# LoRA masks by four products of 32 rows with a constant, in a four-layer transformer kernel

## The chip, the cores and the metric

The kernel runs on one core of a Trainium2 chip. The metric is the device time of one execution in microseconds (us), the median over runs. The engines are called as in the profile: PE (TensorE, matrix products), PEld (its weight loads), DVE (VectorE), ACT (ScalarE), POOL (GpSimd) and SP (SyncE, which issues the DMAs).

## The reference

The reference is four layers; each adds a gated attention-like part and a gated feed-forward part to `x` of 32 x 64 tokens by 256 features (2048 tokens). What matters here is the feed-forward part of the first layer, a gated network with routed LoRA experts (8 experts, the best 2 for each token, rank 16):

```python
gate_base, up_base = xf @ Wg.T, xf @ Wu.T            # 256 -> 704
base_out = jax.nn.silu(gate_base) * up_base @ Wd.T
probs = jax.nn.softmax(xf @ Wr.T, axis=-1)           # 8 experts
topw, topi = jax.lax.top_k(probs, 2)
expert_w = jnp.sum(jax.nn.one_hot(topi, 8) * topw[..., None], axis=1)
for e in range(8):                                   # a scan
    g_lora = xf @ Ag[e].T @ Bg[e].T * 2.0            # rank 16
    u_lora = xf @ Au[e].T @ Bu[e].T * 2.0
    h = jax.nn.silu(gate_base + g_lora) * (up_base + u_lora)
    acc += (h @ Ad[e].T @ Bd[e].T * 2.0) * expert_w[:, e, None]
x = x + jnp.tanh(g_ffn[0]) * (base_out + acc)
```

The kernel computes only the two chosen experts of each token: all 8 x 16 = 128 inner rows of `Ag` and `Au` are computed in one product, and a mask over these 128 rows keeps the rows of the first or of the second expert. A second pair of masks carries the weights for the way out.

## The kernel before

All activations `x` stay on the core as 16 tiles of 128 tokens. The layers are eight blocks: `block0` (a recurrence, by scans on DVE), `block1` (the routed network above), `block2` (a convolution), `block3` (a ternary network), `blocks45` and `block6`, `block7`. Blocks 0 and 1 run together: they work on chunks of two, two, four, four and four tiles (`CHUNKS`), and `program` draws pieces of block 0 between the steps of block 1. Up to the end of block 3 the order of the instructions is set by a planner that works from estimated costs, with the order in the program as priority and the free buffers as a limit; from `blocks45` on PE, DVE, ACT and POOL keep the order in which the program is written.

In block 1 a generator `head` prepares a chunk: layer norm, transposes to `xf` (features on partitions, tokens along the row), and `route`, which gives `sel`. `sel` has tokens on partitions and, for each tile, 4 x 8 values: for every expert whether it is the first (`s` = 0) or the second choice, and the two weights. `head` then builds `mt`, four masks of 128 rows by n x 128 tokens, where a row belongs to expert row // 16. Here POOL copies the 32 values of a tile 16 times each to 512 (`ex`, line 411), PE turns them in four transposes (line 415) into a PSUM tile `pm`, and ACT copies it to `mt` (line 416). `ex` has one buffer; `pm` comes from the pool `c.aux` with tag "a", which has two buffers and is used by the other transposes of blocks 0 and 1 as well. Then the products `pz` (line 423, tag "a" too) give the inner rows of gate and up, and DVE multiplies them with the masks to `z` (line 426). The head of the next chunk is stepped by `ahead` in the last eight steps of a chunk; the head of the first chunk is done at once.

The chunk itself: `gated` takes `pg` and `pu` (line 462 for the base, 465 for the LoRA part of each choice) through silu on ACT (468) and a product on DVE (469); then `pa` (509, 524), `po` (515, 532) and `finish` (537, 542), which adds to `x`. The masks come in again in line 527.

Other lines the prediction names: block 0's `bv` (278), scans (282, 287) and `y` (294) with reciprocals (299), its transposes (181); the load of `con`, a table of constants (1792), and of block 1's weights `l0f` (1763, 1764); `_norm` (167) writes `xn`, also in `blocks45`, where `xn` of tile 0 comes from one pool and those of the other tiles from another. In block 6, lines 1559 and 1569 are products of 32-row strips.

Of the kernel before, what the change touches and what calls it, by code (L numbers as in the profile page):

```python
# [17 lines left out]
F32 = mybir.dt.float32  # L18
# [8 lines left out]
P = 128  # L27
# [20 lines left out]
def _offsets(sizes):  # L48
    out, at = {}, 0
    for name, n in sizes:  # L50
        out[name] = (at, at + n)
        at += n
    return out, at
# [11 lines left out]
L2X, L2X_N = _offsets([("wq", 512), ("wo", 512), ("wk", 512), ("wv", 512), ("mask", NT * S), ("bk", 2), ("bq", 2)])  # L65
ROWS, ROWS_N = _offsets([("bv", D), ("bo", D), ("gb", HID), ("vb", HID), ("ob", D)])
CON, CON_N = _offsets(
    [("cos", 256), ("sin", 256), ("had", P), ("pairs", P), ("half", 2), ("tri", 64), ("odd", 2)]
)
L3X, L3X_N = _offsets([("wq", 256), ("wk", 256), ("wv", 128), ("wo", 128), ("bias", 4), ("bo", 1), ("bv", 1)])  # L70

# [1 line left out]
def _v(t, off, name):  # L73
    a, b = off[name]
    return t[:, a:b]
# [52 lines left out]
def _stats(c, pool, i0=0, n=NT, bufs=1, here=False):  # L128

    mv = pool.tile([P, max(n, 4), 2], F32, tag="ln_mv", name="ln_mv", bufs=bufs)[:, :n]  # L130
    for j in range(n):
        _mean(c, pool, mv[:, j, :], i0 + j, here)
    return mv, _inverse(c, pool, mv, "ln", bufs), i0
# [29 lines left out]
def _norm(c, pool, ln, i, bufs=4):  # L163
    mv, rs, i0 = ln
    j = i - i0
    xn = pool.tile([P, D], F32, tag="xn", name="xn", bufs=bufs)
    c.nc.vector.tensor_scalar(xn, c.x[:, i, :], mv[:, j, 0:1], rs[:, j : j + 1], ALU.subtract, ALU.mult)  # L167
    return xn
# [7 lines left out]
def _turned(c, xns, ps, tag):  # L176
    out = []
    for hf in range(2):
        pt = ps.tile([P, 512], F32, tag=tag, name="pt")
        for q in range(len(xns)):  # L180
            c.nc.tensor.transpose(pt[:, q * P : (q + 1) * P], xns[q][:, hf * P : (hf + 1) * P], c.ident)
        out.append(pt)
    return out
# [148 lines left out]
def block1(c):  # L332
# [5 lines left out]
    nc = c.nc  # L338
# [6 lines left out]
    au = _v(w, L0F, "au").rearrange("p (k e) -> p k e", k=2)  # L345
    ad = _v(w, L0F, "ad").rearrange("p (f e) -> p f e", e=P)
    wr = _v(w, L0F, "wr").rearrange("p (k e) -> p k e", k=2)
    bg, bu, bd = _v(w, L0F, "bg"), _v(w, L0F, "bu"), _v(w, L0F, "bd")
    E = 8
    with ExitStack() as es:  # L350
        sm = es.enter_context(c.tc.tile_pool(name="sm1", bufs=1))
        ps = es.enter_context(c.tc.tile_pool(name="ps1", bufs=6, space=PSUM))
        ph = c.aux
        hp = es.enter_context(c.tc.tile_pool(name="hp1", bufs=1))
        tp = es.enter_context(c.tc.tile_pool(name="tp1", bufs=2))
# [37 lines left out]
        def head(i0, n):  # L393

            ln = _stats(c, sm, i0, n, bufs=2)
            yield
            xns = [_norm(c, sm, ln, i0 + q) for q in range(n)]
            yield
            N = n * P
            xf = tp.tile([P, 2, 512], F32, tag="xf", name="xf")  # L400
            pts = _turned(c, xns, ph, "a")
            nc.scalar.copy(xf[:, 0, :N], pts[0][:, :N])
            nc.scalar.copy(xf[:, 1, :N], pts[1][:, :N])
            yield
            sel = route(xf, n)
            yield
            mt = hp.tile([P, 4, 512], F32, tag="mt", name="mt", bufs=2)
            for q in range(n):
                ex = tp.tile([P, 4 * E, 16], F32, tag="ex", name="ex", bufs=1)
                src = sel[:, q, :, :].rearrange("p a e -> p (a e)")  # L410
                nc.gpsimd.tensor_copy(ex, src.unsqueeze(2).to_broadcast([P, 4 * E, 16]))
                exf = ex.rearrange("p a r -> p (a r)")
                pm = ph.tile([P, 4, P], F32, tag="a", name="pm")
                for a in range(4):
                    nc.tensor.transpose(pm[:, a, :], exf[:, a * P : (a + 1) * P], c.ident)
                nc.scalar.copy(mt[:, :, q * P : (q + 1) * P], pm)
                if q % 2:
                    yield
            z = {}
            for m, wt in (("g", ag), ("u", au)):  # L420
                pz = ph.tile([P, 512], F32, tag="a", name="pz")
                for k in range(2):
                    nc.tensor.matmul(pz[:, :N], wt[:, k, :], xf[:, k, :N], start=k == 0, stop=k == 1)
                for s in range(2):
                    z[m, s] = hp.tile([P, 512], F32, tag=f"z{m}{s}", name=f"z{m}{s}", bufs=2)
                    nc.vector.scalar_tensor_tensor(z[m, s][:, :N], pz[:, :N], 2.0, mt[:, s, :N], ALU.mult, ALU.mult)
                z[m, 2] = hp.tile([P, 512], F32, tag=f"z{m}2", name=f"z{m}2", bufs=2)
                nc.gpsimd.tensor_tensor(z[m, 2][:, :N], z[m, 0][:, :N], z[m, 1][:, :N], ALU.add)
            ready.append((xf, mt, z))
            yield  # L430
# [3 lines left out]
        for _ in head(*CHUNKS[0]):  # L434
            pass
        for t, (i0, n) in enumerate(CHUNKS):
            N = n * P
            xf, mt, z = ready.pop(0)
            nxt = head(*CHUNKS[t + 1]) if t + 1 < len(CHUNKS) else None
            step = 0  # L440

# [71 lines left out]
            for q in range(n):  # L513
                for f in range(NF):
                    ins = nc.tensor.matmul(  # L515
                        pos[q % 2][:, q // 2], h[2][:, f, q * P : (q + 1) * P], wd[:, f, :],
                        start=f == 0 and q < 2, stop=False, skip_group_check=True,
# [3 lines left out]
                if q == 1:  # L521
                    for s in range(2):
                        rows = slice(s * S, (s + 1) * S)
# [6 lines left out]
            for q in range(n):  # L530
                rows, tc = slice(q % 2 * S, (q % 2 + 1) * S), slice(q * P, (q + 1) * P)
# [403 lines left out]
def blocks45(c, kw):  # L935
# [6 lines left out]
    nc = c.nc  # L942
# [4 lines left out]
    half = _v(c.con, CON, "half")  # L947
    pairs = _v(c.con, CON, "pairs")
# [13 lines left out]
    with ExitStack() as es:  # L962
        es4 = es.enter_context(ExitStack())
        sm4 = es4.enter_context(c.tc.tile_pool(name="sm4", bufs=1, side="right"))
        t4 = es4.enter_context(c.tc.tile_pool(name="te4", bufs=1, side="right"))
# [9 lines left out]
        lns, more = [_stats(c, sm4, 0, 4, bufs=2)], []  # L975
# [58 lines left out]
        @op  # L1034
        def xn(a):
            a.x = c.x[:, a.i, :]
            a.xn = _norm(c, t4, lns[a.i // 4], a.i, bufs=2)

        @op
        def gbo(a):  # L1040
# [377 lines left out]
        t4 = es4.enter_context(c.tc.tile_pool(name="tp4", bufs=2, side="right"))  # L1418
# [317 lines left out]
def program(tc, a, out):  # L1736
    nc = tc.nc
    with ExitStack() as es:
# [45 lines left out]


        first, second = block0(c), block1(c)
        next(first)
        early, conv_w = ExitStack(), ExitStack()
# [105 lines left out]
def _constants():  # L1894

    con = np.zeros((P, CON_N), np.float32)
    inv = (np.float32(1.0) / np.float32(10000.0) ** (np.arange(0, 8, 2, dtype=np.float32) / np.float32(8))).astype(np.float32)
    f = (np.arange(D, dtype=np.float32)[:, None] * inv[None, :]).astype(np.float64)
    a = CON["cos"][0]
    b = CON["sin"][0]  # L1900
    o = CON["odd"][0]
    for j in range(4):
        for h in range(2):
            rows = slice(32 * j + 8 * h, 32 * j + 8 * (h + 1))
            con[rows, a : a + D] = np.cos(f[:, np.arange(8) % 4]).T
            con[rows, b : b + D] = np.sin(f[:, np.arange(8) % 4]).T * np.repeat([-1.0, 1.0], 4)[:, None]
            con[32 * j + 16 + h, a : a + D] = 1.0
            con[rows, o + h] = 1.0
            con[32 * j + 16 + h, o + h] = 1.0
    had = np.ones((1, 1), np.float32)  # L1910
    while had.shape[0] < P:
        had = np.block([[had, had], [had, -had]])
    con[:, slice(*CON["had"])] = had
    p = np.arange(P)
    con[:, slice(*CON["pairs"])] = p[:, None] // 64 == p[None, :] // 64
    con[:, slice(*CON["half"])] = p[:, None] % 32 // 16 == np.arange(2)[None, :]
    e = np.arange(8)
    con[:, slice(*CON["tri"])] = (e[None, :] < e[:, None]).reshape(1, 64)
    return con

# [20 lines left out]
def _layout(i):  # L1941
# [37 lines left out]
    out["wu"] = np.concatenate([i["L0_xattn_w"].reshape(2, P).T, i["L0_xattn_u"].reshape(2, P).T], axis=1)  # L1979
    out["l3f"] = np.concatenate([_chunks(i["L3_ffn_W1"].T), _chunks(i["L3_ffn_W3"].T), _chunks(i["L3_ffn_W2"].T)], axis=1)  # L1980
    out["con"] = _constants()
    return {n: np.ascontiguousarray(v) for n, v in out.items()}

# [13 lines left out]
```

## Time and profile before

| | |
|---|---|
| median of 3 runs | 1341.95 us (1341.44 to 1345.03) |
| the profiled execution | 1339.78 us, of which the span of the instructions is 1337.9 us |
| granted TensorE clock, mean | 0.973 |
| `ex` copies, POOL, line 411 | 16, 804 ns mean (602 to 1423 ns) |
| mask transposes, PE, line 415 | 64, 273 ns median from start to end, pipelined |
| `mt` copies, ACT, line 416 | 16, 586 ns median |
| last products of block 1 (line 537) | start at 360.61 us |

Times in the profile are microseconds from the start of the span. A line of a timeline has the start, the length, the engine, the source line, the operation, what it writes and reads with shapes, how many, and in square brackets the engine's idle time before it and who ended it. Matmuls overlap in the array, so the time that PE gives to one is seen from start to start, not from its length. An f32 product is two instructions; a transpose is one.

### The profile page before, as it was taken

To read this page: it belongs to the slowest core of one execution; us is meant where nothing else is said; L and a number is where in the kernel's file an instruction comes from. 1 tells how busy PE (TensorE), PEld (TensorE's weight loads), DVE (VectorE), ACT (ScalarE), POOL (GpSimd) and SP (SyncE) were. 2 spreads that over 40 slices of the span, in tenths; PEclk is the share of its full clock that TensorE was granted. 3 is DMA by queue.
4 is the path that set the end of the run, shared out by engine and by line. 5 is a ranking of instruction groups with operands and counts; after the bars stand their busy time and mean duration, and the time that the engine had idled before them with its cause. 6 is when DMAs were issued, how large, how long until landed. Compare 5 with 4: busy or idle time off the path is not lost.

```text
span 1337.9 us, 21457 instructions
## 1 busy us (share of the span) xinstructions
PE 1193.0 (89%) x8342; PEld 722.0 (54%) x8342; DVE 906.7 (68%) x2175; ACT 618.6 (46%) x1046; POOL 460.3 (34%) x505
## 2 busy tenths in 40 slices
PE   0789899899999999987878976799999999999999
PEld 0667345354533367765656653455555555555665
DVE  6588777645349897558999996587787887532111
ACT  2563634322131154657989981455555555511110
POOL 3332606210113233325777775233234335000000
PEclk9899999999999998989999996899999999999999
DMA  6000000100142120000000010110000000000000
GB/s 216 20 1 16 1 0 1 63 1 1 46 175 95 49 87 1 1 1 1 2 2 2 1 65 1 37 59 1 2 1 1 2 1 1 1 8 9 16 16 16
DMA packets 10294, 34.14 MB, mean 26 GB/s; under 512 B 1360, under 2 KB 5968, under 8 KB 8528
## 3 DMA queue, kind: packets, MB, share of 16 engines
q1 hardware_dynamic: 10192, 32.76, 6.9%
q8 instruction: 66, 1.08, 0.3%
q14 instruction: 36, 0.29, 0.1%
HBM read 30.66 MB, written 2.10 MB: 24 GB/s over the span
## 4 chain that ended last, share of the span: by engine, by line
PE 58%; DVE 27%; POOL 5%; ACT 4%; issue 4%; DMA 2%; SPq 0%; DVEq 0%; POOLq 0%; ACTq 0%
PE pw L1559 6%; PE po L1582 5%; PE pp L1569 4%; PE po L1731 4%; PE pu L1721 4%; PE pg L1721 4%; PE pc L610 3%; PE pu L462 2%; PE pg L462 2%; PE pu L465 2%; PE pa L509 2%; DVE xn L167 2%; PE po L515 2%; PE pg L465 2%; PE pp L1502 1%
## 5 line engine op out<-in xcount | busy, mean ns | idle before, releaser
L1575 DVE TENSOR_REDUCE mx<-pp 128x4 f32<-128x1024 f32 x128 | 155.9, 1218 | 40.7 <-PE pp L1569 40.3
L1561 ACT ACTIVATE e<-pw 128x1024 f32<-128x1024 f32 x128 | 130.9, 1024 | 111.1 <-PE pw L1559 67.0
L1559 PE MATMUL pw<-qs,kb 32*128 32x256 f32 x1024 | 144.5, 402 | 7.5 <-DVE qs L1546 4.4
L1569 PE MATMUL pp<-kb,q 32*128 32x512 f32 x512 | 147.3, 658 | 4.3 <-POOL q L1530 4.0
L1559 PEld LDWEIGHTS pw<-qs,kb 32*128 32x128 f32 x1024 | 87.2, 185 | 51.9 <-issue 29.2
L468 ACT ACTIVATE sg<-pg 128x512 f32<-128x512 f32 (+1 forms) x75 | 37.8, 512 | 116.6 <-PE pg L462 51.1
L610 PE MATMUL pc<-xw,wb 64*64 64x512 f32 x768 | 90.3, 601 | 0.2 <-DVE x L542 0.2
L1724 DVE TENSOR_TENSOR h<-pu,sg 128x512 f32<-128x512 f32 x32 | 22.1, 692 | 80.8 <-PE pu L1721 80.8
L1723 ACT ACTIVATE sg<-pg 128x512 f32<-128x512 f32 x32 | 19.1, 597 | 122.8 <-PE pg L1721 122.7
L469 DVE TENSOR_TENSOR h<-pu,sg 128x512 f32<-128x512 f32 (+1 forms) x75 | 42.5, 573 | 48.1 <-PE pu L462 29.4
L1524 POOL TENSOR_TENSOR k<-t,t 128x512 f32<-128x512 f32 x16 | 20.3, 1267 | 147.9 <-DVE t L1509 147.9
L1582 PE MATMUL po<-e,va 128*32 128x256 f32 x1024 | 69.2, 388 | 1.8 <-ACT e L1561 1.8
L764 POOL TENSOR_TENSOR acc<-acc,sq 128x512 f32<-128x512 f32 x28 | 38.3, 1369 | 68.6 <-ACT sq L763 67.3
L1721 PE MATMUL pg<-xf,wa 128*128 128x512 f32 x128 | 60.3, 592 | 0.0
L1721 PE MATMUL pu<-xf,wa 128*128 128x512 f32 x128 | 60.3, 592 | 0.0
L610 PEld LDWEIGHTS pc<-xw,wb 64*64 64x64 f32 x768 | 30.1, 133 | 53.4 <-issue 52.6
L1731 PE MATMUL po<-hb,h 128*128 128x256 f32 x256 | 55.9, 379 | 0.0
L1731 PEld LDWEIGHTS po<-hb,h 128*128 128x128 f32 x256 | 48.6, 190 | 8.3 <-issue 1.9
L110 DVE BATCH_NORM_STATS2 ln_st<-x 128x6 f32<-128x256 f32 x112 | 44.4, 409 | 10.9 <-POOL x L1611 7.2
L1582 PEld LDWEIGHTS po<-e,va 128*32 128x32 f32 x1024 | 26.9, 110 | 44.0 <-issue 17.4
L1509 DVE SCALAR_TENSOR_TENSOR t<-pp,wb,con 128x512 f32<-128x512 f32 x64 | 45.0, 744 | 8.3 <-PE pp L1502 8.3
L1527 POOL TENSOR_SCALAR kb<-k,con 128x512 f32<-128x512 f32 x32 | 49.7, 1564 | 1.6
(342 smaller groups left out, 2947.0 us busy)
## 6 DMA issues: line engine op xcount, KB each, us to landing
w<-in_l2f SPq DMA_DIRECT2D x12, 512.0 KB, 3.9
wa<-in_l0f SPq DMA_DIRECT2D x2, 1828.0 KB, 12.7
wa<-in_l1f SPq DMA_DIRECT2D x2, 1536.0 KB, 9.3
wa<-in_l3f SPq DMA_DIRECT2D x2, 1536.0 KB, 8.0
wb<-in_conv SPq DMA_DIRECT2D x1, 2048.0 KB, 7.5
ctx<-in_ctxT SPq DMA_DIRECT2D x2, 1024.0 KB, 6.0
ctx<-in_ctxN SPq DMA_DIRECT2D x2, 1024.0 KB, 5.9
out<-x SPq DMA_DIRECT2D x16, 128.0 KB, 1.7
```

Of the source, the lines that this page charges most:

```text
L462: nc.tensor.matmul(p, wt[:, k, fc], xf[:, k, :N], start=k == 0, stop=False, skip_group_check=True)
L465: nc.tensor.matmul(p, wt[:, fc], z[m, s][:, :N], start=False, stop=s == 1, skip_group_check=True)
L610: nc.tensor.matmul(pcs[h][to], w[rows, k, m, h, :], xw[rows, k, h, :, Z - m : Z - m + 32], start=m == 0, stop=m == Z)
L1509: nc.vector.scalar_tensor_tensor(t[r], pp[:, :, r, :], bias[:, n, r : r + 1], f, ALU.add, ALU.mult)
L1527: nc.gpsimd.tensor_scalar(kb[:, :, h, :], k, odd[:, h : h + 1], None, ALU.mult)
L1559: nc.tensor.matmul(pw[:, jj, k, :], w.k[rows, h, k * P : (k + 1) * P], w.qs[rows, :], start=True, stop=True)
L1561: nc.scalar.activation(e, pw, AF.Exp, scale=scale)
L1569: nc.tensor.matmul(pp[:, jj], p.q[rows, t * P : (t + 1) * P], p.k[rows], start=True, stop=True)
L1575: nc.vector.tensor_reduce(p.mx[:, t, i0 : i0 + 2, 16:18], pp, AX.X, ALU.max, negate=True)
L1582: nc.tensor.matmul(po[strip(j), :], a.v[:, k, 2 * j + h, :], a.e[h, j][:, k, :], start=k == 0, stop=k == 1)
L1721: nc.tensor.matmul(p, wt[:, k, fc], xf[:, k, :], start=k == 0, stop=k == 1)
L1731: nc.tensor.matmul(po, h[:, f, q * P : (q + 1) * P], c.w2h[:, f, :], start=f == 0, stop=f == NH - 1)
```

## The change

The 32 values of a tile are copied four times by POOL (to `four`, 4 x 32 = 128 per tile) instead of 16 times. One transpose per tile turns these 128 into 128 rows, so that each strip of 32 partitions holds the 32 values of all tokens of the chunk; ACT copies the turned tile back into `four` (called `rows`). Then for each of the four masks one product of 32 rows, `spread[strip]` (32 x 128) with `rows[strip]` (32 x n x 128 tokens), spreads the 8 values of that mask to the experts' 128 rows. `spread` is a new constant of 128 columns in `con`, so `con` is larger by 64 KB. Each product goes to a PSUM tile of its own with tag "a" and is copied to `mt[:, a]` by ACT. `head` yields after the second and the fourth product. In `blocks45`, `xn` of tile 0 has one buffer instead of two.

```diff
 CON, CON_N = _offsets(
-    [("cos", 256), ("sin", 256), ("had", P), ("pairs", P), ("half", 2), ("tri", 64), ("odd", 2)]
+    [("cos", 256), ("sin", 256), ("had", P), ("pairs", P), ("half", 2), ("tri", 64), ("odd", 2), ("spread", P)]
 )
...
+    spread = _v(c.con, CON, "spread")
...
             sel = route(xf, n)
             yield
+
+            four = tp.tile([P, 4, 4, 4 * E], F32, tag="four", name="four", bufs=1)[:, :n]
+            for q in range(n):
+                src = sel[:, q, :, :].rearrange("p a e -> p (a e)")
+                nc.gpsimd.tensor_copy(four[:, q], src.unsqueeze(1).to_broadcast([P, 4, 4 * E]))
+            pt = ph.tile([P, 4, P], F32, tag="a", name="pt4")
+            for q in range(n):
+                nc.tensor.transpose(pt[:, q, :], four[:, q].rearrange("p s r -> p (s r)"), c.ident)
+            rows = four.rearrange("p q s r -> p (q s r)")
+            nc.scalar.copy(rows, pt[:, :n].rearrange("p q t -> p (q t)"))
             mt = hp.tile([P, 4, 512], F32, tag="mt", name="mt", bufs=2)
-            for q in range(n):
-                ex = tp.tile([P, 4 * E, 16], F32, tag="ex", name="ex", bufs=1)
-                src = sel[:, q, :, :].rearrange("p a e -> p (a e)")
-                nc.gpsimd.tensor_copy(ex, src.unsqueeze(2).to_broadcast([P, 4 * E, 16]))
-                exf = ex.rearrange("p a r -> p (a r)")
-                pm = ph.tile([P, 4, P], F32, tag="a", name="pm")
-                for a in range(4):
-                    nc.tensor.transpose(pm[:, a, :], exf[:, a * P : (a + 1) * P], c.ident)
-                nc.scalar.copy(mt[:, :, q * P : (q + 1) * P], pm)
-                if q % 2:
+            for a in range(4):
+                strip = slice(32 * a, 32 * (a + 1))
+                pm = ph.tile([P, 512], F32, tag="a", name="pm")
+                nc.tensor.matmul(pm[:, :N], spread[strip, :], rows[strip], start=True, stop=True)
+                nc.scalar.copy(mt[:, a, :N], pm[:, :N])
+                if a % 2:
                     yield
...
-            a.xn = _norm(c, t4, lns[a.i // 4], a.i, bufs=2)
+            a.xn = _norm(c, t4, lns[a.i // 4], a.i, bufs=2 if a.i else 1)
...
+    con[:, slice(*CON["spread"])] = p[:, None] % 32 == p[:, None] // 32 * 8 + p[None, :] // 16
```

## The prediction

> **What bounds the kernel now.** I read the page first, then busy time by stage, then the mask tiles with their waits, then the timeline and the chain of waits around the five places where masks are made. The page's engine list says who could be late:
>
> ```profile
> span 1337.9 us, 21457 instructions
> PE   1193.0 (89%) x8342; PEld 722.0 (54%) x8342; DVE 906.7 (68%) x2175; ACT 618.6 (46%) x1046; POOL 460.3 (34%) x505
> ```
>
> An average, so I cut block 1 and the end of block 0 out. The view by stretch lists start:end, length, and busy us (instructions) of PE, PEld, DVE, ACT, POOL, then the granted clock:
>
> ```profile
> 31.00:45.00 14.00, 12.32 (x48) 9.90 (x48) 6.05 (x30) 4.18 (x8) 1.64 (x3) 1.00 0.20 70
> 75.00:95.00 20.00, 16.70 (x88) 13.21 (x87) 18.30 (x49) 10.47 (x18) 6.30 (x10) 1.00 0.00 1
> 127.00:160.00 33.00, 27.68 (x107) 14.90 (x105) 25.40 (x46) 19.18 (x30) 20.35 (x25) 1.00 0.00 0
> 190.00:224.00 34.00, 29.63 (x119) 17.89 (x118) 23.74 (x40) 15.03 (x26) 20.20 (x18) 0.95 0.00 1
> 224.00:262.00 38.00, 38.00 (x99) 17.61 (x97) 23.78 (x54) 8.96 (x15) 6.24 (x5) 1.00 0.15 56
> 300.00:363.00 63.00, 63.00 (x201) 33.23 (x200) 24.81 (x55) 14.36 (x25) 5.93 (x7) 1.00 0.00 0
> ```
>
> The five heads lie at 31 to 45 (head 0, two tiles), 88 to 94 (head 1, two), 138 to 149 (head 2, four), 205 to 214 (head 3, four) and 279 to 286 (head 4, four). Around heads 0 and 4, and from 224 on, PE is full: PE time added there is time of the kernel. Around heads 1 to 3 PE has gaps (3.3 us in 75 to 95, 5.3 in 127 to 160, 4.4 in 190 to 224), because block 0 still runs on POOL, DVE and ACT. What a faster POOL part can give is in the waits on the copies it makes:
>
> ```profile
> its engine sat idle before it (us, times) until:
>   POOL ex L411: 23.3, 19
> ```
>
> These 23.3 us are PEld (15.5) and PE (7.8) together, from the list of waits; only PE's 7.8, and 1.8 more noted on a memset behind a copy, are gaps in the array. All 9.6 lie in heads 1 to 3. Head 4 is the clean loop without block 0:
>
> ```profile
> 280.46 0.61 POOL L411 COPY ex<-sel 128x512 f32<-128x512 f32 x1 [0.84 <-PE pm L415]
> 281.13 0.66 PE L415 MATMUL pm<-ident,ex 128*128 128x128 f32 x4
> 281.62 1.02 PE L509 MATMUL pa<-h,wa 128*128 128x512 f32 x2
> 281.82 0.59 ACT L416 COPY mt<-pm 128x512 f32<-128x512 f32 x1 [0.87 <-PE pm L415]
> 282.59 0.66 PE L415 MATMUL pm<-ident,ex 128*128 128x128 f32 x4
> ```
>
> A round lasts 1.46 us (281.13 to 282.59). PE gives 0.49 of it to four transposes (to 281.62) and 0.86 to `pa` products that fill the wait; 0.1 is lost. POOL's copy is hidden by the filler.
>
> **The change part by part, PE.** Out go 16 groups of four transposes, 16 x 0.49 = 7.8 us of PE: 1.96 in a head of four tiles, 0.98 in one of two. In come one group per head (0.49 for four tiles, 0.27 for two) and four products. An f32 product with 512 columns is two instructions; a pair of L465 takes 0.86 on the chain (for instance at 246.51), with 256 columns 0.43 (109.35). Fewer rows need not be cheaper, so one product alone costs 0.86. Products on different strips can overlap: in block 6, from 903.70 to 904.83, four instructions of 512 and eight of 256 columns on 32-row strips start and end, 4 x 0.43 + 8 x 0.215 = 3.44 us of work in 1.13. How many overlap here is set by the two PSUM buffers of tag "a": the first two products come free together, when the copy of `rows` ends (its buffer is released then); the third waits for the ACT copy of the first, the fourth for that of the second, 0.59 us apart. I take one overlapped pair (0.90) and two single (1.72): a head of four tiles 0.49 + 2.62 = 3.11, so +1.15; bounds -0.34 (all four in 1.13) and +1.97 (all apart). A head of two: 0.27 + 0.45 + 0.86 = 1.58, so +0.6, bounds 0 and +1.0.
>
> The products also change the array's tile shape. The nearest rows are the 64-row products of block 1:
>
> ```profile
> 287.97 4.48 PE L515 MATMUL po<-wa,h 128*128 128x256 f32 x20
> 292.38 1.13 PE L524 MATMUL pa<-ht,wa 64*128 64x512 f32 x4
> 293.44 4.58 PE L515 MATMUL po<-wa,h 128*128 128x256 f32 x20
> 297.95 1.13 PE L532 MATMUL po<-wa,ht 64*128 64x256 f32 x8
> ```
>
> Twenty instructions of 256 columns at 0.215 (L537: eight in 1.72, 226.60 to 228.32) are 4.30; here the next shape starts after 4.41 and 4.51. A switch thus costs 0.1 to 0.2 us. With fillers put between the products a head has two to six switches: 0.2 to 1.2 us, I take 0.7 (0.5 in head 0). The Trainium skill, "TensorEngine Tiling (Array Packing)", Tiling Modes, speaks against the change here: a change of tiling mode drains the engine; it gives no figure, the rows above do. The Trainium skill, "TensorE: Matmul & The Clock Gate", Part 3, gives 3.07x for four 32-row products side by side, and block 6 shows 3.44/1.13 = 3.0; by it alone, ignoring the two buffers, each head of four tiles would gain 0.34 us instead of losing 1.15, and my sum of +2.6 would be about -0.4.
>
> **POOL.** Out go 16 copies (12.9 us busy, 804 ns mean, 614 undisturbed). In come 16 of a quarter of the elements. No row has that shape: the 128x128 memset of `ident` (0.20) is the low bound, the full copy (0.61) the high one; I take 0.25, nearer the memset, since the element count is the same. Lock-out by DVE remains: the first copy of heads 1, 2 and 3 takes 1.42, each while a DVE scan of L282 (1.23 to 1.24 us) runs. The scan starts just behind `sel` and the first small copy meets it too, so PE's first wait (2.6, 1.7 and 1.7 us) stays.
>
> **ACT.** Out: 16 copies of 0.586 = 9.4 us. In: per head of four tiles five of 0.586, per head of two five of 0.37 (the 128x256 copy of L402): 8.8 + 3.7 = 12.5, so +3.1. Hidden where ACT is under half busy, but longer in sequence: after the transposes come `rows`, product, copy, and two more copies before `pz` gets a buffer. In head 4 `pz` would start about 0.7 us later; `z` isn't read before 307.88, so that costs nothing while `po` and `pa` products fill PE, and up to 0.7 if they don't. In heads 1 and 2 the activations of block 0 queue behind these copies on ACT; POOL's `y` (L294) waits for them.
>
> **The rest at nothing.** `con` grows by 128 x 128 x 4 B = 64 KB, some 0.3 us at 205 GB/s; it and the `l0f` behind it are loaded while block 0 alone runs; first use of `l0f` at 33.81 waits for ACT (`xf`), not for the load. If uncovered: +0.3. `xn` with one buffer is asked for tile 0 alone, whose pool is replaced before tile 1: no wait. The head of two tiles yields once more, which moves its `pz` one step of an order that a planner rearranges anyhow.
>
> **Sum by head.**
> - Head 0: PE full and block 0's next transposes (44.84) are behind it: +0.6 +0.5 = +1.1 (0 to +2).
> - Head 1: PE's extra 1.1 lies in its gap. The third scan (91.58, 1.61 us) no longer meets a copy: -0.37 against 1.24; a second small copy ahead of `bv` L278: +0.25. Together -0.1 (-1 to +1).
> - Head 2, where the chain runs through POOL:
>
> ```profile
> 138.71 1.36 issue
> 140.07 0.80 POOL bv L278
> 140.87 1.25 issue
> 142.12 0.61 POOL ex L411
> 142.79 0.66 PE pm L415 x4
> 143.48 0.59 ACT mt L416
> ...
> 146.24 0.61 POOL ex L411
> ```
>
>  "issue" is the locked-out copy. The copy at 146.24 goes (-0.6), three small ones come ahead of `bv` (+0.6), and ACT's 1.5 us wait for the second group may shrink: I take -1.0, together -1.0 (-2.7 to +1).
> - Head 3: PE +1.15, switches +0.7, gaps of 0.7 between later groups gone: +1.15 (-1.5 to +3).
> - Head 4: +1.15 +0.7, four losses of 0.1 gone: about +1.5 (+0.4 to +3).
>
> 1.1 - 0.1 - 1.0 + 1.15 + 1.5 = +2.6. The profiled execution took 1339.78 (span 1337.9 and 1.9 around it): 1342.4. The median of the three runs is 2.2 above it: 1344.5. What a measurement here can tell from no change is about 0.3%, 4 us; this forecast is inside it.
>
> **Rivals.** *Gaps closed* (0.18): the shorter POOL part frees block 0 in heads 1 to 3. Of the 9.6 us of gaps two thirds go (6.4), the products pair up on all strips (3 x 0.34 = 1 more): 7 us faster, near 1335. For it: the chain in head 2. Against: the first wait of each head, 6 of the 9.6, is DVE's lock-out.
>
> *Product by product* (0.40): every product stands alone between fillers. Head 4: 1.97 + 1.2, less 0.3, = 2.9; head 3 1.97 + 1.2 - 0.7 = 2.5; head 0 1.0 + 1.2 = 2.2; with -0.1 from head 1 and nothing from head 2: +7.5, near 1349.5. It decides against me from the point where fewer than two products per head run side by side and ACT's copies for block 0 stand between the mask copies. For it: PE's order in head 4 already alternates transposes with fillers, and ACT in heads 1 to 3 is shared.
>
> *Nothing to see* is my own case (0.42): the parts cancel to within 4 us. The reordered plan alone may give or take some 2 us, as PE has 30 us of gaps between 31 and 363.
>
> The range is 1336.5 to 1351: it holds the slower rival's middle and goes 1.5 us short of the faster one's, which leaves out about 1 in 10 at each end. My own case alone spans 1338 to 1346. Faster by over 0.3%: 0.18; within: 0.42; slower by over: 0.40.
>
> **What the next profile would show.** Right: small copies near 0.25 us with the first still over 1 us in heads 1 to 3; products of 32 rows of which the first two start within 0.1 us; POOL busy down by some 6 us (three first copies near 1.2, thirteen at 0.25, for 12.9), ACT up by 3; the last L537 products starting about 3 us later than 360.61. Wrong: products alone with 0.2 us around each; or `y` L294 and the reciprocals after head 2 more than 2 us earlier; or a shift made after 363, which no step of mine has.

## The result and the profile after

The changed kernel takes 1353.84 us (median of 4 runs, 1352.54 to 1354.33) against 1342.47 (4 runs, 1341.44 to 1345.03): ratio 1.0087, 95% interval 1.0069 to 1.0105. It is slower by 11.4 us, outside the range given. The profiled execution took 1354.33 us. Its engine list:

```profile
span 1352.5 us, 21425 instructions
PE 1211.5 (90%) x8334; PEld 727.6 (54%) x8334; DVE 906.6 (67%) x2175; ACT 620.8 (46%) x1055; POOL 458.4 (34%) x505
```

Of the 64 transposes 16 are left and 20 products have come, which the prediction had at some 4.7 us more of PE before the switches. PE is busy for 18.5 us more (1193.0 before; a second profile of the unchanged kernel, `before2` below, has 1200.9, so some 8 of them are chance). POOL saved 1.9 us in place of some 6. A busy time that grows by more than the work that came in says: look at the clock.

The two traces are compared by the instructions that both have: the start after less the start before, its median in the quiet stretches between the heads. The differences from one stretch to the next are what each head costs:

| us | head 0 | head 1 | head 2 | head 3 | head 4 | block 1 in all |
|---|---|---|---|---|---|---|
| predicted | +1.1 | -0.1 | -1.0 | +1.15 | +1.5 | +2.6 |
| changed kernel | +1.1 | +4.4 | -1.5 | +4.1 | +3.2 | +12.3 |
| changed kernel, second profile (`again`) | +0.7 | +4.2 | -1.5 | +4.9 | +2.8 | +11.0 |

The last column is the shift at 300 to 360 us, with the 0.9 us in it (-0.2 in the second profile) that lay ahead of head 0. The last product of block 1, `po` with `zg`, starts at 374.5 in place of 362.2. Head 1 in the timeline after (start, length, engine, line, what; in brackets idle time before it and who ended it):

```profile
89.84 1.23 DVE L282 TENSOR_TENSOR_SCAN e<-a,e 128x520 f32<-128x520 f32 x1
90.05 2.29 POOL L412 COPY four<-sel 128x128 f32<-128x128 f32 x2 [0.67 <-DVE sel L391]
90.99 1.26 DVE L287 TENSOR_TENSOR_SCAN bv<-a,bv 128x520 f32<-128x520 f32 x1
91.21 0.33 PE L415 MATMUL pt<-ident,four 128*128 128x128 f32 x1 [2.74 <-POOL four L412]
92.39 0.48 PE L415 MATMUL pt<-ident,four 128*128 128x128 f32 x1 [0.85 <-POOL four L412]
...
94.51 1.22 PE L422 MATMUL pm<-four,con 32*128 32x256 f32 x4
97.67 1.22 PE L422 MATMUL pm<-four,con 32*128 32x256 f32 x4
99.84 3.27 PE L430 MATMUL pz<-xf,wa 128*128 128x256 f32 x8
```

And the same head before:

```profile
89.52 0.66 PE L415 MATMUL pm<-ident,ex 128*128 128x128 f32 x4 [2.62 <-POOL ex L411]
90.01 1.03 PE L537 MATMUL po<-wa,zg 128*128 128x256 f32 x4
90.88 0.59 PE L462 MATMUL pg<-xf,wa 128*128 128x256 f32 x2
92.15 0.65 PE L415 MATMUL pm<-ident,ex 128*128 128x128 f32 x4 [0.68 <-POOL a L274]
92.64 1.97 PE L423 MATMUL pz<-xf,wa 128*128 128x256 f32 x8
```

Two scans stand back to back on DVE, and each small copy ends only when the scan beside it has ended: the two take 1.10 and 1.24 us, against 0.29 to 0.30 for the ten copies of this kernel that meet no scan. Before, one copy was caught; the first group of transposes and 1.3 us of other products followed it while POOL went on. Now PE does a single transpose between two waits, and the products come after two more steps. The eight `pz` instructions took 1.8 us (92.64 to the next start at 94.45) and take 3.1 now. The view by stretch shows why (start:end, length, busy PE, PEld, DVE, ACT, POOL, granted clock). The clock changes only on a grid of 3.41 us that runs on from stretch to stretch, so I cut along it (a "window" below is one such piece of 3.41 us); first before, then after:

```profile
85.04:88.45 3.41, 1.86 (x8) 1.30 (x8) 3.34 (x13) 3.40 (x8) 1.74 (x2) 1.00 0.02 5
88.45:91.86 3.41, 1.95 (x10) 1.45 (x10) 3.31 (x5) 2.02 (x4) 3.41 (x3) 1.00 0.00 0
```

```profile
88.98:92.39 3.41, 0.33 (x1) 0.14 (x1) 3.20 (x6) 1.24 (x3) 2.74 (x4) 1.00 0.00 0
92.39:95.80 3.41, 3.41 (x10) 1.93 (x10) 0.48 (x1) 1.55 (x4) 1.14 (x2) 0.50 0.00 0
95.80:99.21 3.41, 3.41 (x9) 1.93 (x10) 2.29 (x3) 1.94 (x6) 1.62 (x1) 0.50 0.00 0
99.21:102.62 3.41, 3.41 (x9) 2.69 (x9) 2.17 (x3) 3.36 (x6) 1.78 (x5) 0.50 0.00 0
```

Before, the gap of 2.62 us lies across a border, and each window still has 1.9 us of work. After, one window has 0.33, and the clock is 0.50 in the next three, 10.2 us. PE is busy for all of them, but the first two hold the narrow products; only the third, with `pz`, is followed by 1.00. The second profile has the same, from 90.5 to 100.8. The Trainium skill, "TensorE: Matmul & The Clock Gate", Part 1, tells of a clock that halves after an idle window of about 3.4 us and is released by a busy one. The length agrees with these rows; the release doesn't: here two windows in which PE is busy throughout, or nearly so, are not followed by 1.00.

In head 3 the same pair of copies is caught, and no filler stands between the second product and the third:

```profile
211.34 0.33 PE L415 MATMUL pt<-ident,four 128*128 128x128 f32 x1 [1.34 <-POOL four L412]
212.53 0.80 PE L415 MATMUL pt<-ident,four 128*128 128x128 f32 x3 [0.85 <-POOL four L412]
...
214.13 1.13 PE L422 MATMUL pm<-four,con 32*128 32x512 f32 x4
215.92 2.13 PE L422 MATMUL pm<-four,con 32*128 32x512 f32 x4 [0.67 <-ACT mt L423]
```

The clock is 0.50 from 218.7 to 222.1, under `pz`. In head 4, where nothing is caught, the products themselves leave PE waiting:

```profile
288.75 1.02 PE L516 MATMUL pa<-h,wa 128*128 128x512 f32 x2
289.71 1.13 PE L422 MATMUL pm<-four,con 32*128 32x512 f32 x4
291.50 1.61 PE L422 MATMUL pm<-four,con 32*128 32x512 f32 x4 [0.67 <-ACT mt L423]
293.30 5.40 PE L430 MATMUL pz<-xf,wa 128*128 128x512 f32 x8 [0.19 <-ACT mt L423]
```

Again 0.50, from 293.8 to 297.2 (in the second profile the clock does not fall here).

### The profile page after: what moved, and what is told of

Read it like the earlier page. It is cut to its first block, busy times and chain, and to the rows that moved or that the text cites. A ratio compares the mean times of both kernels' runs of the same rounds, so it can differ in the third digit from the quotient of the medians.

```text
span 1352.5 us, 21425 instructions
## 1 busy us (share of the span) xinstructions
PE 1211.5 (90%) x8334; PEld 727.6 (54%) x8334; DVE 906.6 (67%) x2175; ACT 620.8 (46%) x1055; POOL 458.4 (34%) x505
## 4 chain that ended last, share of the span: by engine, by line
PE 59%; DVE 26%; ACT 5%; POOL 4%; issue 3%; DMA 2%; SPq 0%; DVEq 0%; POOLq 0%; ACTq 0%
PE pw L1566 6%; PE pp L1576 5%; PE po L1589 4%; PE po L1738 4%; PE pu L1728 4%; PE pg L1728 4%; PE pc L617 4%; PE pg L469 2%; PE pu L469 2%; DVE xn L167 2%; PE po L522 2%; PE pu L472 2%; PE pg L472 2%; PE pa L516 2%; PE pp L1509 1%
```

## The experiments

The theory: block 0's scans hold the small copies, the wait and the narrow products halve the clock, and the masks' longer chain passes it on. The rivals: the products are simply dearer, the longer constants delay the start, or the later blocks' order is at fault. All times are medians beside runs of the kernel before on the same chip. The heads' costs come from one profile each, against the first profile of before, and the profiled execution need not lie at the median: it took 1347.48 us in `full_rows` (the fastest of its six runs), 1351.34 in `four_act` and 1341.86 in `act23`.

| us | heads 0, 1, 2, 3, 4 | block 1 | time | ratio, 95% interval |
|---|---|---|---|---|
| `con_pad` | -0.9, 0, 0, 0, -0.1 | -0.2 | 1342.54 | 0.9998 (0.9984 to 1.0011) |
| `full_rows` | +1.8, +2.6, -1.5, +2.5, +1.7 | +6.7 | 1352.12 | 1.0077 (1.0056 to 1.0099) |
| `sel4` | +0.2, +1.2, -3.8, -0.7, +1.7 | -0.6 | 1343.27 | 1.0005 (0.9994 to 1.0017) |
| `act_ex` | +1.0, +4.6, -4.0, -1.5, +0.4 | +1.5 | 1344.18 | 1.0014 (0.9995 to 1.0032) |
| `mix23` | +0.9, 0, -3.8, -0.3, +1.1 | -2.4 | 1342.91 | 1.0019 (1.0003 to 1.0035) |
| `four_act` | +1.2, +0.1, +1.9, -2.2, +1.7 | +2.9 | 1348.79 | 1.0047 (1.0028 to 1.0065) |
| `no_prod` | +0.8, +8.2, +3.4, +0.8, -0.5 | +12.3 | 1352.50 | 1.0076 (1.0050 to 1.0103) |
| `one_copy` | +0.3, +1.9, -2.4, +1.7, +6.2 | +6.9 | 1349.64 | 1.0054 (1.0040 to 1.0068) |
| `mix2` | +0.5, 0, -3.8, -1.6, -0.2 | -5.7 | 1337.96 | 0.9980 (0.9964 to 0.9996) |
| `act23` | -0.2, +0.7, -3.3, -3.0, +0.6 | -5.0 | 1338.60 | 0.9975 (0.9962 to 0.9989) |

**What is chance: `again`, `before2`, `con_pad`.** The first two are unedited; `con_pad` is

```diff
-    [... ("tri", 64), ("odd", 2)]
+    [... ("tri", 64), ("odd", 2), ("spread", P)]
-            a.xn = _norm(c, t4, lns[a.i // 4], a.i, bufs=2)
+            a.xn = _norm(c, t4, lns[a.i // 4], a.i, bufs=2 if a.i else 1)
```

> The changed kernel once more, unedited, for a second profile: does the later start (kp copies at 11.96 us against 11.07 before), the loss in heads 1, 3 and 4 (+4.4, +4.1, +3.7 us) and the late part (+4 us after 700 us) come again? If they belong to the kernel, each repeats within 0.3 us. If the start or the late part is chance, they differ by 0.5 us or more from the first profile.

> The kernel before once more for a second profile. If its first profile (span 1337.9 us) was at the fast end of its runs (1337 to 1346 us), this one is 2 to 5 us longer, and the difference lies behind 490 us, in other stretches of half clock; block 1 (to 300 us) repeats within 0.5 us. Rival: the profile repeats throughout, and the later 2 to 4 us of the changed kernels belong to them.

> The kernel before, with the constants 128 columns longer (never used) and xn's one buffer; the order of all engines stays. Theory of the load: the longer constants share the DMA engines with the two gate loads, the gate that ACT's first Tanh waits for lands about 1 to 1.8 us later than 8.54 us, block 0 starts 0.9 us later, and the whole takes about 1343.4 us (ratio 1.0007). Rival, chance or the new work: no shift at 12 us, the time of before.

`again` took 1355.97 us. The heads repeat within 0.3 us, but for heads 0 and 4 (0.4) and head 3 (0.8); the start doesn't. `before2` took 1342.12 with a span of 1340.3: block 1 within 0.7 us, and 3.1 us later from there to the end, in other stretches at 0.50. It starts 0.5 us later and makes 1.0 us good in head 0, `con_pad` likewise 0.8 and 0.9, so the cost of head 0 is known to 1 us only. `con_pad` is at no change in time. So the load and `xn` cost nothing that can be told, the start was chance, and the first profile of before, at 1339.78, was a quick one: of the 14.6 us between the first two profiles about 2.5 are not the change's. Single medians of before lay between 1340.95 and 1343.57.

**Rows of the products: `full_rows`.**

```diff
-                nc.tensor.matmul(pm[:, :N], spread[strip, :], rows[strip], start=True, stop=True)
+                nc.tensor.matmul(pm[:, :N], spread, rows, start=True, stop=True)
```

> The changed kernel, in which each of the four products takes all 128 rows in place of a strip of 32 (the masks' values are then wrong: four sums in place of four strips); the order of all engines stays. Theory of rows: products over 32 rows count as little work for TensorE's clock, and with them and the waits between them the granted clock falls to 0.50 for 4 us behind the products of head 3 (218.2 to 222) and head 4 (293.3 to 297.8). With 128 rows the clock there stays at 1.00, pz's eight products take 3.6 us in place of 5.3, and the pairs take 1.9 us in place of 1.13: head 3 gains 0.3 to 1 us, head 4 gains 0.5 to 1 us, heads 0 to 2 lose 0.5 to 1.5 us each, the whole within 2 us of 1353.8. Rival, waits alone: the clock falls as in the changed kernel, and every head loses 0.5 to 1.5 us by the longer pairs, the whole about 1358 us.

In the profile the products got longer and block 1 shorter, by 5.6 us. Head 1's half clock lasted one window (92.8 to 96.2) in place of three. Head 4:

```profile
285.83 3.76 PE L422 MATMUL pm<-four,con 128*128 128x512 f32 x8
289.43 3.68 PE L430 MATMUL pz<-xf,wa 128*128 128x512 f32 x8
```

Clock 1.00 behind the products of heads 3 and 4; `pz` takes 3.68 in place of 5.40. In head 3 it had fallen earlier instead, 208.8 to 212.2, through the waits. So in this profile the clock behind the products went as the theory of rows said. The time does not confirm it: this is the fastest of six runs (1347.48 to 1355.39 us), the median is only 1.7 us below that of the changed kernel, and the intervals of the two ratios overlap. A clock that falls in one profile need not in the next (`again` has no fall behind head 4's products), so the rows were measured by themselves.

**Rows alone: `rep32`, `rep128`.** Each product four times over, in strips of 32 rows or over all 128:

```diff
+                for _ in range(4):
-                nc.tensor.matmul(pm[:, :N], spread[strip, :], rows[strip], start=True, stop=True)
+                    nc.tensor.matmul(pm[:, :N], spread[strip, :], rows[strip], start=True, stop=True)   # rep128: spread, rows
```

> The changed kernel with each of the four products made four times over (16 products of 32 rows in a row per head, the values unchanged), for the granted clock alone. Theory of rows: products over 32 rows don't hold TensorE's clock, so in heads 2, 3 and 4, where the 16 products last 6 us or more without a gap, the clock falls to 0.50 within them and products get twice as long. Rival: a busy TensorE keeps its clock whatever the rows, 1.00 throughout the 16 products, and only idle time lets it fall.

> As the run before, TensorE's order the same, but each product over all 128 rows (the masks' values are then wrong). Both theories: the clock stays at 1.00 through the 16 products of heads 2, 3 and 4, each product 0.43 us for 512 columns and pass or 0.86 in all. If the clock falls here as with 32 rows, the number of rows isn't the cause.

They took 1389.61 and 1389.47 us. By stretch, with heads 0, 1, 2 and 3 of 32 rows:

```profile
42.40:45.80 3.40, 3.40 (x25) 2.99 (x21) 0.00 (x0) 1.12 (x3) 0.00 (x0) 1.00 0.00 0
45.80:49.20 3.40, 3.40 (x9) 2.31 (x8) 0.66 (x2) 0.37 (x1) 0.00 (x0) 0.50 0.00 0
97.00:103.80 6.80, 6.80 (x26) 5.82 (x25) 3.94 (x4) 5.04 (x9) 3.11 (x5) 0.50 0.00 0
153.81:172.40 18.59, 18.59 (x34) 8.01 (x33) 13.24 (x10) 8.05 (x12) 14.22 (x15) 0.50 0.00 0
235.60:245.80 10.20, 10.20 (x34) 4.81 (x33) 6.29 (x4) 6.87 (x13) 7.93 (x6) 1.00 0.00 0
```

and heads 0, 1 and 2 of 128 rows:

```profile
41.00:47.90 6.90, 6.90 (x33) 6.10 (x33) 0.43 (x1) 1.12 (x3) 0.00 (x0) 1.00 0.00 0
97.40:100.70 3.30, 3.30 (x10) 2.58 (x9) 2.77 (x3) 1.37 (x3) 1.74 (x2) 0.50 0.00 0
100.80:106.20 5.40, 5.40 (x27) 4.75 (x26) 1.29 (x2) 5.02 (x9) 1.54 (x4) 1.00 0.00 0
154.63:156.00 1.37, 1.37 (x4) 0.67 (x3) 1.13 (x2) 1.35 (x3) 0.94 (x1) 0.74 0.00 0
156.00:168.70 12.70, 12.70 (x31) 5.55 (x30) 10.33 (x7) 6.53 (x10) 12.46 (x15) 1.00 0.00 0
```

Neither text was right in full. In both kernels the products of heads 1 and 2 run at half clock from their start (in head 1 of `rep32` from 0.4 us behind it). Head 1 is the clean pair: one window with 3.0 us of products over 128 rows (97.3 to 100.7) is followed by 1.00, while two windows filled by products over 32 rows alone (97.0 to 103.8) are not, and the clock stays at 0.50 until 110.6, through one window of `pz`. In head 2 with 128 rows it ends at the next border, 155.3, in a window that held 2.6 us of other products too; with 32 rows it stays for the 18.6 us of products and one window of `pz` more. With 256 columns (head 0 of `rep32`) a window filled with 32-row products even lets a full clock fall (42.4 to 45.8); with 512 (heads 3 and 4) they hold it for 10 us. So a narrow product counts for less than a wide one, and doesn't bring a halved clock back.

The windows of the other fourteen profiles (before and after twice each, and the ten of the table) agree, from the first record of the clock in each, near 40 us, to 330 us. Of 62 windows at full clock that were followed by 0.50, 58 had at most 1.78 us of PE work; none with less than 1.46 held. The other four had 2.56, 2.75, 2.75 and 3.16 us, and they are head 4 and head 3 of after, head 2 of `four_act` and head 3 of `mix23` (202.0 to 205.4), where 32-row products are most of the work. Nor are these products alone in it: in `one_copy` three windows from 268.0 to 278.2, at least 3.1 us busy each, did not release the clock, and 1.9 us of their work are transposes and 3.3 us the 8-column products of `route`. In that span before has six windows at 0.50, after eleven in both profiles, `full_rows` seven, `sel4` and `mix2` five. One costs PE 1.7 us where PE is full, so the five more of after cost up to 8.5.

**The locked-out copies: `sel4`, `four_act`, `one_copy`.** `sel4` writes the values at their strips' places in a tile zeroed once, and has no small copy (the constant is set to match); `four_act` gives the copies to ScalarE; `one_copy` makes one GpSimd copy per chunk:

```diff
 # sel4
-            sel = tp.tile([P, 4, 4, E], F32, tag="sel", name="sel")[:, :n]
+            sel = wide[:, :n, :, :E]          # wide: [P, 4, 4, 4 * E]
-                nc.gpsimd.tensor_copy(four[:, q], src.unsqueeze(1).to_broadcast([P, 4, 4 * E]))
-                nc.tensor.transpose(pt[:, q, :], four[:, q]..., c.ident)
+                nc.tensor.transpose(pt[:, q, :], wide[:, q]..., c.ident)
 # four_act
-                nc.gpsimd.tensor_copy(four[:, q], src.unsqueeze(1).to_broadcast([P, 4, 4 * E]))
+                nc.scalar.copy(four[:, q], src.unsqueeze(1).to_broadcast([P, 4, 4 * E]))
 # one_copy
-            for q in range(n):
-                ...                           # the copy of one block
+            src = sel.rearrange("p q a e -> p q (a e)")
+            nc.gpsimd.tensor_copy(four, src.unsqueeze(2).to_broadcast([P, n, 4, 4 * E]))
```

> The changed kernel without GpSimd's small copies: the routing values are written at their strips' places in a tile that is zeroed once, and the transposes read that tile. The order of the engines changes with it. Theory of the locked-out copy: TensorE's waits for the copies (2.74 and 0.85 us in head 1, 1.37 and 0.85 in head 2, 1.34 and 0.85 in head 3) go, head 1 keeps its clock (0.50 from 92.7 to 102.5 in the changed kernel), and the whole is 6 to 10 us shorter, 1344 to 1348 us. Rival, the chain that stays (transpose, copy, product, copy): the next wait takes the place of the removed one, at most 2 us gained, 1352 or more.

> The changed kernel with the small copies made by ScalarE in place of GpSimd, every other step of the chain (copy, transpose, copy, product, copy) kept. Theory of the locked-out copy: a ScalarE copy isn't held by VectorE's scans, so TensorE's waits of 2.74 and 0.85 us in head 1, 1.37 and 0.85 in head 2, 1.34 and 0.85 in head 3 fall below 1.6 us each head, and most of the 11 us comes back as in the run without small copies: 1343 to 1347 us. Rival, the longer chain: with all its five steps still there the kernel stays at 1350 us or above.

> The changed kernel with one small copy on GpSimd for a whole chunk in place of one for each block of 128 tokens; TensorE's order the same. Theory of the second wait: the first wait (2.74 us in head 1) is that of the kernel before (2.62), where the clock stood; what is new is the second copy held behind the next scan, 0.85 us more with 0.2 us of work between. With one copy the second wait goes in heads 1, 2 and 3, TensorE has its fillers right behind the transposes, the clock stays at 1.00 through the products of head 1, and 4 to 8 us come back: 1346 to 1350 us. Rival: the first wait alone lets the clock fall (and a copy of twice or four times the size waits for as much), so the second wait goes and the clock still halves behind head 1: 1351 us or more.

`sel4` is 1.0 us above the kernel before beside it, in place of 11.4, with the products still there; the order of POOL and DVE around the heads changes with it. Its head 1:

```profile
89.10 0.41 PE L414 MATMUL pt<-ident,wide 128*128 128x128 f32 x2 [1.58 <-DVE wide L394]
...
90.30 0.70 PE L421 MATMUL pm<-four,con 32*128 32x256 f32 x4
...
92.00 0.70 PE L421 MATMUL pm<-four,con 32*128 32x256 f32 x4
...
93.16 1.98 PE L429 MATMUL pz<-xf,wa 128*128 128x256 f32 x8
```

One wait, on DVE; clock 1.00 from 87 to 103; `pz` 6.7 us earlier than after. `four_act` keeps every step, and its copies take 0.29 to 0.30 us each, in head 2 beside a scan (140.02 to 141.26); in heads 1 and 3 the scan starts behind them. Head 1 costs 0.1 in place of 4.4:

```profile
89.58 0.53 PE L415 MATMUL pt<-ident,four 128*128 128x128 f32 x2 [1.27 <-ACT four L412]
```

Head 2 had two windows at 0.50 under the last products and `pz` (147.0 to 153.9) instead. Its time is 6.1 us above before: 1348.79 is above the theory's 1347 and below the rival's 1350. In its profile block 1 ends 2.9 us late and 8.8 us more come behind it, where `before2` has 3.1; these are not explained. `one_copy` takes away the second wait alone:

```profile
88.95 0.44 PE L414 MATMUL pt<-ident,four 128*128 128x128 f32 x2 [2.84 <-POOL four L411]
```

Heads 1 to 3 cost 2.6, 0.9 and 2.4 us less than after. The clock still falls in head 1, for two windows (90.5 to 97.3) in place of three. So the rival was right that the first wait can do it, the theory in the sum, 1349.64. Head 4 was at 0.50 from 268.0 to 281.6 there, a fall that began in a wait for `xn`, as in before (269.3 to 272.7), and lasted four windows in place of one, the three named above and one more.

**Without the products: `no_prod`.**

```diff
-                nc.tensor.matmul(pm[:, :N], spread[strip, :], rows[strip], start=True, stop=True)
-                nc.scalar.copy(mt[:, a, :N], pm[:, :N])
+                nc.scalar.copy(mt[:, a, :N], pt[:, :n].rearrange("p q t -> p (q t)"))
```

> The changed kernel without the four products (the masks' values are then wrong: each mask row is copied from the transposed values themselves); GpSimd's small copies, the transposes and the copies to the masks stay. Theory of the wait: the loss of heads 1 and 3 comes ahead of the products, so the wait of 2.7 us in head 1 stays and so does most of its loss; what goes is the products' own time and the waits for their buffers, about 2 us in heads 2 to 4 and 1 in heads 0 and 1, 8 us in all, or 1346 us. Rival, the products carry the loss by their 32 rows: without them the clock stays up behind head 1 too and the whole is that of before or faster, 1336 to 1342 us.

1352.50, 6 us above what the theory said and far from the rival's. The waits stay as they are in after, and the clock with them: 0.50 from 88.8 to 95.6.

```profile
89.52 0.48 PE L415 MATMUL pt<-ident,four 128*128 128x128 f32 x1 [2.73 <-POOL four L412]
90.71 0.47 PE L415 MATMUL pt<-ident,four 128*128 128x128 f32 x1 [0.71 <-POOL four L412]
90.97 1.91 PE L427 MATMUL pz<-xf,wa 128*128 128x256 f32 x4
```

The loss needs no product: this kernel has sixteen windows at 0.50 up to 330 us, where after has eleven. The planner's order around the heads is another one here (POOL's `y` starts later, and a second half clock comes at 105.9), so head 1's +8.2 is not to be set against +4.4 term by term.

**Where the gain of head 2 comes from, and a faster kernel: `act_ex`, `mix23`, `mix2`, `act23`.** `act_ex` and `act23` are the kernel before with its large copies on ScalarE, in all heads or in heads 2 and 3; `mix23` and `mix2` use `sel4`'s products in these heads or in head 2 alone.

```diff
 # act23, on the kernel before
-                nc.gpsimd.tensor_copy(ex, src.unsqueeze(2).to_broadcast([P, 4 * E, 16]))
+                copy = nc.scalar.copy if i0 in (4, 8) else nc.gpsimd.tensor_copy
+                copy(ex, src.unsqueeze(2).to_broadcast([P, 4 * E, 16]))
```

> The kernel before, with the four large copies of each head made by ScalarE in place of GpSimd. Theory of the locked-out copy: TensorE's waits for them (2.62 and 0.68 us in head 1, 1.69, 1.10 and 1.11 in head 2, 1.66, 0.18 and 0.51 in head 3) come from GpSimd's place behind VectorE's scans; a ScalarE copy of this size takes 0.59 us, so the waits fall by half or more and the whole is 3 to 5 us shorter, 1338. Rival: the copies then stand in ScalarE's queue behind the scans' activations and the eviction of the masks, each head loses 0.5 to 1 us, 1344 to 1347.

> The products without GpSimd's copies (values written at their strips' places) in heads 2 and 3 alone; heads 0, 1 and 4 by large copies and transposes as before. By the stages of the run with products in all heads and no small copies, against before: head 1 +1.2, head 2 -3.8, head 3 -0.7, head 4 +1.7 us. If the stages are independent, heads 2 and 3 alone give -4.5 us, 1338 us. Rival: what is gained there is waited for at the next stage or lost to the clock, 1341 to 1343 us.

> The products without GpSimd's copies in head 2 alone, all other heads as before. By the stages: head 2 -3.8 us, all other stages as before, 1338 us. Rival: a gain in block 1 isn't kept to the end, because the order planned for the later blocks or the halves of the clock take it back, 1341 to 1343 us, as with heads 2 and 3.

> The kernel before, with the large copies of heads 2 and 3 alone made by ScalarE, those of heads 0, 1 and 4 by GpSimd; no products anywhere. By the stages of the run with ScalarE's copies in all heads: head 2 -4.0 us, head 3 -1.5 us. Theory of the locked-out copy: the gain of head 2 (-3.8 us with products) comes from GpSimd's copies leaving the chain and not from the products, so head 2 gains 3.5 us or more here too, and the whole is 1337 to 1339 us. Rival: it is the products that gain in head 2, head 2 gains less than 1.5 us here, 1341 or more.

Head 2 gains 3.8 with products and no small copies, 4.0 and 3.3 with no products and the large copies on ScalarE: the gain belongs to GpSimd's copies leaving the chain. `act_ex` lost it again in head 1 (+4.6, where its rival had 0.5 to 1). Its runs fall into two groups, five from 1337.6 to 1338.9 us, where the theory had it, and seven from 1344.1 to 1347.9; the profile is of the second group. `mix23` kept its block 1 gain of 2.4 in the profile, but not in the median; its head 4 had 6.8 us at 0.50 (263.4 to 270.3), 7.3 us came behind block 1, and why is not settled. `mix2` (1337.96 against 1342.66) and `act23` (1338.60 against 1343.57) are faster than both kernels, by little: the ratios are 0.9980 and 0.9975, with intervals just below 1. `act23` does so without any of the change; its head 2:

```profile
139.94 0.66 PE L416 MATMUL pm<-ident,ex 128*128 128x128 f32 x4
142.16 0.60 PE L416 MATMUL pm<-ident,ex 128*128 128x128 f32 x4
144.63 0.66 PE L416 MATMUL pm<-ident,ex 128*128 128x128 f32 x4 [0.16 <-ACT ex L412]
```

against waits of 1.69, 1.10 and 1.11 us in this head before.

## Why the prediction was wrong

The forecast was 1344.5 us, +2.6 from the heads; the runs showed 1353.84 and +12.3 (+11.0 in the second profile). Heads 1, 3 and 4 hold most of the difference: +4.4, +4.1 and +3.2 against -0.1, +1.15 and +1.5.

- **POOL, the term that failed.** "Three first copies near 1.2, thirteen at 0.25": six were held, two in each of heads 1 to 3, at 1.10 and 1.24, since the scans come in pairs (L282, L287). The undisturbed copy was 0.29 to 0.30. All 16 took 9.3 us of POOL, not 6.9 (3 x 1.2 + 13 x 0.25). The step "a second small copy ahead of `bv` L278: +0.25" in head 1 was 1.24. Before, the second large copy had to wait until PE had freed `ex`, and in head 1 it came behind the first pair of scans (91.48); small copies without such a wait run straight into them. A copy held in second place was to be seen before: the fourth of head 3 took 1.19 us (210.73).
- **"PE's first wait stays"** was right (2.74, 1.37 and 1.34 us against 2.62, 1.69 and 1.66). What stood behind it was overlooked: the old chain needed one copy to go on, the new one needs all copies of the chunk, then a transpose, a copy, a product and a copy. By `sel4` against after, one profile each, the small copies with the half clocks that follow them cost 3.3, 2.3 and 4.8 us in heads 1, 2 and 3: 10.4 of the 12.3.
- **Clock, a term that was missing.** The sum took every PE price at full clock. Its own views show 0.95 from 190 to 224, and they leave out 262 to 300, where before has 0.96 and PE idles for 3.6 us: "from 224 on, PE is full" did not hold just ahead of head 4. The 1.00 of its first stretch, 31 to 45, is no reading up to 40.62, where the trace has its first record of the clock: four products of 256 columns (L462, 37.39 to 39.09) take 0.43 us each there, against 0.215 in L537. That waits may fill a window and that 32-row products don't release the clock had no term. What the rows cost in the whole stays open: with 128 rows block 1 is 5.6 us shorter in the one profile, the median time 1.7. The term of the copies and that of the clock overlap: without the small copies most of the falls are gone too.
- **Head 4, +1.5 (to +3).** +3.2 and +2.8 in all, with a half clock behind the products in the first profile and one window more of it ahead of them in the second; +1.7 in `sel4` and `four_act`, which have neither. The PE work, the pairs and the two PSUM buffers were sized about right: pairs did come, the third product waited 0.67 us for its buffer.
- **Heads 0 and 2, the load, `xn`, ACT.** +1.1 and +0.7 against +1.1 for head 0, near by luck where chance alone moves 1 us; -1.5 against -1.0 for head 2, though two copies were held there too; no change for the load and `xn`; ACT busy +2.2 against +3.1.
- **The sign of later shifts.** Those behind 363 us come in `before2` and `con_pad` too, so they belong to no step; the 2.2 us between profile and median had been put into the sum.
- **The rival "product by product"** ended nearest in time (1349.5) and not by its mechanism: the products came in adjacent pairs, 1.13 us for two of 512 columns. It priced neither copies nor clock.

## What to carry to other kernels

Making a step four times smaller on an engine that is held by another one saves little while it is still held once per instruction: count the instructions that can meet the holder, not their elements. Ask of a chain that is cut into stages whether the first stage's first part used to be enough to go on; if it now needs the whole, the waits that were spread among fillers come in a row. And where a busy time rises without more work, read the granted clock in the stretch before looking for dearer instructions; differences of a few us need the clock's own scatter from a second profile of the same kernel.

## What the runs showed of the hardware

- The granted clock changes on a grid of 3.41 us; in the fourteen profiles above every window at full clock with less than 1.46 us of PE work was followed by 0.50, and of those with more than 1.78 only the four in which 32-row products were most of the work. Where the grid lies differs from run to run, so the same gap of 2.6 us in head 1 costs nothing in before (1.86 and 1.95 us of work) and a window in `act23` (0.78 us, then 0.50 from 90.1 to 93.5). The same program ran between 1334.51 and 1347.11 us.
- Products over 32 rows count for less in that: 18.6 us of them did not release a halved clock, and in head 1 two windows full of them did not, where one with 3.0 us of products over 128 rows did.
- A GpSimd copy of 128x128 beside VectorE's scans takes 1.10 or 1.24 us against 0.29, with its size counting for little: one of 128x256 took 1.21 and one of 128x512 1.42. The Trainium skill, "GPSIMD Engine Reference", Specifications, says that GpSimd shares its SBUF interfaces with VectorE and contends with instructions of two SBUF inputs; the scans are such, and the rows agree. ScalarE made the same 128x128 copy in 0.29 to 0.30 us beside a scan (head 2 of `four_act`) and one of 128x512 in 0.62 (head 2 of `act23`).
